# Interleaving a second stream with an LSTM: per-block multipliers and applies ahead of residual squares and statistics

## The chip, the cores and the metric

The kernel runs on one core of one Trainium2 chip. The metric is the device time of the program in microseconds (us). Before the change it took 1949.37 us, the median of three runs (1946.18 to 1950.16).

## The reference, cut to what matters

A batch of 128 graphs with 64 nodes and 256 features goes through four layers, each `x = x + layer(relu(layernorm(x)))` on the residual stream `x`: a batch-normed graph convolution, a graph convolution followed by LSTMs, an attention, and a masked attention. The change is inside the second layer:

```python
h = relu(layernorm(x))
u = relu(adj @ (h @ Wg0 + bg0)); u = relu(adj @ (u @ Wg1 + bg1))      # two graph convolutions
for p in range(1, 5):                                                 # four LSTMs, one after another
    g = x_t @ Wih[p-1].T + h @ Whh[p-1].T + bias                      # p steps per window of p nodes
    c = sigmoid(f) * c + sigmoid(i) * tanh(gg);  h = sigmoid(o) * tanh(c)
    u[:, last node of each window] = h of the last step
x = x + u
```

Each LSTM overwrites nodes that the next one reads, so the four follow each other.

## The kernel before, in words

All values are fp32. The 8192 rows (graph, node) of `x` are cut into 16 chunks of 512 rows. In the LSTM stage two chunks make a block, and the loop `for sc in range(last + 1)` of L1045 goes over the eight blocks. The input of a block's LSTMs is a tile `hT`, features on partitions and columns ordered by node and graph.

**The LSTM stream.** `lstm` (L676) builds matmuls on TensorE (PE) into PSUM banks, gates on ScalarE (ACT), cell and state updates on VectorE (DVE). For p = 1 a block is done in two parts of 512 columns. A part has six PSUM banks (gates i, g and o, called 0, 2 and 3, by two feature halves c) and 12 products of 512 columns (L790), which the profile shows as 24 matmuls, four to a bank. The banks have the tags y, z and x, two banks each, so part 1 reuses the banks of part 0, and p = 2 those of part 1: a matmul that opens a bank waits until ACT has read it. ACT reads a bank by a sigmoid or tanh (`first_acts`, L769). DVE then multiplies (`first_cell`, L775), ACT takes the tanh of the cell (L776), and DVE writes the new state into `hT` (`new_state`, L729). The ACT order of a part is gate 0, gate 2, two tanhs of the cell, gate 3. p = 2 runs its first products on halves of the nodes, 24 matmuls of 256 columns each: the first 24 need part 0's states alone, the other 24 part 1's.

**The other stream.** Every `yield` of `lstm` is a place, numbered n = 0 to 21 in a block: n = 0 and 1 lie in and after part 0 of p = 1, n = 2 and 3 in and after part 1, n = 4 inside the products of p = 2, n = 5 after its first step. At a place the loop takes one unit of other generators (L1069, L1070), in the order in which `units` entered them. The generators are:

- `residual` (L930) of the two chunks of the previous block: unit 0 transposes 32x32 squares on DVE (L936, four instructions into `hm`) and writes them to DRAM (`put`, L239); unit 1 reads them back into the dead `hT` (`get`, L246, four DMAs); unit 2 adds them to the residual `xs` (`add_squares`, L276).
- `convolutions` (L622) of the two chunks of the next block, 14 units: unit 0 scales and transposes (L542, L630), writes, reads back and loads `xs`; unit 1 adds squares to `xs` (L276); unit 2 takes the layernorm statistics (L165, L166, and a reciprocal root on GpSimd, POOL, L99 and L100); units 3 and 4 make the multiplier `nmr` on DVE (L183) and apply the layernorm on ACT in two halves (L185, two instructions each); unit 5 is a matmul with the adjacency (`agg_b`, L206), unit 6 copies its banks (L647), unit 7 multiplies by the weights (L557), and so on.
- `ahead` (L995) of the previous block's chunks, which prepares the next layer: put, read back, statistics (at n = 21), and, for the second chunk, in the following block under the name `LATE`: two applies (units 3 and 4: L183, then L185 into `h`) and unit 5, squares and put (L264, L239).

The order of all five engines is written by hand (`manual_schedule`, L1042): each engine runs its instructions in the order of the code, and a wait holds whatever is behind it on that engine. The DMAs here are issued from SyncE (SP), in order too. The tiles `hm`, `h2` and `nm` share one tag with three buffers.

## Time and profile before

| | value |
|---|---|
| time, median of 3 | 1949.37 us (1946.18 to 1950.16) |
| profiled execution: time, span, mean granted PE clock | 1950.89 us, 1949.1 us, 0.997 |
| PE busy | 1918.5 us, 98% of the span |
| DVE, ACT, POOL busy | 1143.4 us (59%), 947.3 us (49%), 367.8 us (19%) |
| blocks 2 to 6: start of p = 1 on PE | 608.41, 770.75, 931.37, 1091.94, 1254.20 us |

The page of the profile gives busy times by engine, and groups of instructions by source line with the idle time of the engine just before them and what ended it. A row of the timeline has the start, the length and the engine, then the source line, the operation, the tiles and the count of what was merged; a bracket at its end is the idle time of that engine just before, with its releaser. The waits view sums the idle time of one engine by line and releaser. The table by stretches gives busy time of each engine and the granted PE clock, 1.00 being full speed.

### The profile page before, as it was taken

The numbers are of one execution on the slowest core, as the hardware profiler recorded it, in microseconds if no ns is written. First come the engines' busy times: TensorE is split into PE (matmuls) and PEld (weight loads), VectorE is DVE, ScalarE is ACT, GpSimd is POOL, SyncE is SP. The second block draws the span as 40 slices with busy tenths as digits, with TensorE's granted clock in tenths as the row PEclk, the third lists the DMA queues.
The fourth block names the chain that finished last, engine by engine and source line by source line (L and its number), as shares of the span: only waits on it lengthen the run. The fifth ranks groups of instructions, "written<-read, shape, count | busy, mean of one in ns | idle before, by whom it ended". The sixth has DMA issues, their size and how long they took to land.

```text
span 1949.1 us, 37871 instructions
## 1 busy us (share of the span) xinstructions
PE 1918.5 (98%) x14839; PEld 1437.6 (74%) x14839; DVE 1143.4 (59%) x3000; ACT 947.3 (49%) x2120; POOL 367.8 (19%) x525
## 2 busy tenths in 40 slices
PE   9999999999999999999999999999999999999998
PEld 5444456896896898699689689879969966666665
DVE  6644454556556656655755754665555566566675
ACT  5654434455455455455544545535554544333443
POOL 2105211211211211121121121112112111111121
PEclk9999999999999999999999999999999999999999
DMA  4216712125324522531632542253144244444432
GB/s 135 61 36 228 281 34 80 67 82 191 124 82 160 176 82 80 177 109 65 213 112 82 179 157 82 101 169 108 58 150 129 86 150 122 131 134 138 140 117 82
DMA packets 109057, 238.23 MB, mean 122 GB/s; under 512 B 11216, under 2 KB 73168, under 8 KB 108880
## 3 DMA queue, kind: packets, MB, share of 16 engines
q1 hardware_dynamic: 108128, 234.47, 36.3%
q8 instruction: 117, 1.92, 0.4%
q0 software_dynamic: 320, 1.05, 0.2%
q14 instruction: 60, 0.49, 0.1%
q10 hardware_dynamic: 432, 0.30, 0.0%
HBM read 168.93 MB, written 66.85 MB: 121 GB/s over the span
## 4 chain that ended last, share of the span: by engine, by line
PE 88%; DVE 4%; ACT 3%; DMA 2%; issue 1%; POOL 1%; SPq 0%; DVEq 0%; ACTq 0%; POOLq 0%
PE x L826 22%; PE g L790 13%; PE z L826 11%; PE y L826 6%; PE z L369 6%; PE v L1095 5%; PE p_q L1102 5%; PE z L352 5%; PE p_k L1102 3%; PE u L571 3%; PE v L557 3%; DMA far_y<-ym 1%; PE agg_c L206 1%; PE s L1269 1%; PE o L1316 1%
## 5 line engine op out<-in xcount | busy, mean ns | idle before, releaser
L835 DVE TENSOR_TENSOR gates<-gates,x 128x128 f32<-128x128 f32 (+2 forms) x384 | 119.6, 323 | 344.9 <-PE x L826 343.0
L826 PE MATMUL x<-xd,wset 128*128 128x128 f32 (+2 forms) x1280 | 285.3, 311 | 0.1
L826 PE MATMUL x<-hd,wset 128*128 128x128 f32 (+2 forms) x1152 | 247.1, 303 | 0.0
L826 PEld LDWEIGHTS x<-xd,wset 128*128 128x128 f32 x1280 | 202.4, 190 | 17.0 <-DVE gates L835 3.0
L790 PE MATMUL g<-hT,wset 128*128 128x256 f32 (+2 forms) x744 | 191.8, 415 | 12.5 <-ACT gates L769 11.4
L718 ACT ACTIVATE gates<-gates,bias 128x256 f32<-128x256 f32 (+4 forms) x384 | 170.4, 491 | 66.5 <-DVE gates L835 63.7
L884 POOL TENSOR_TENSOR gates<-gates 128x512 f32<-128x512 f32 (+2 forms) x48 | 74.9, 1560 | 647.0 <-ACT gates L718 624.3
L826 PEld LDWEIGHTS x<-hd,wset 128*128 128x128 f32 x1152 | 185.3, 191 | 4.9
L790 PEld LDWEIGHTS g<-hT,wset 128*128 128x128 f32 x744 | 142.8, 195 | 60.6 <-ACT gates L769 17.5
L769 ACT ACTIVATE gates<-g,bias 128x512 f32<-128x512 f32 (+2 forms) x240 | 136.0, 608 | 103.7 <-PE g L790 100.4
L790 PE MATMUL g<-hT,wih 128*128 128x512 f32 x384 | 166.4, 593 | 0.0
L826 PE MATMUL z<-hs,wset 128*128 128x128 f32 (+2 forms) x768 | 154.2, 303 | 0.0
L832 ACT COPY gates<-y 128x128 f32<-128x128 f32 (+2 forms) x192 | 54.1, 293 | 205.6 <-PE y L826 205.1
L790 PEld LDWEIGHTS g<-hT,wih 128*128 128x128 f32 x384 | 72.5, 190 | 87.5 <-issue 82.9
L826 PEld LDWEIGHTS z<-hs,wset 128*128 128x128 f32 x768 | 119.9, 191 | 3.3
L352 PE MATMUL z<-agg,w_sb 128*128 128x512 f32 x256 | 114.1, 599 | 1.5 <-DVE agg L337 1.5
L775 DVE TENSOR_TENSOR cell<-gates 128x512 f32<-128x512 f32 (+2 forms) x80 | 50.0, 648 | 106.2 <-ACT gates L769 106.0
L369 PE MATMUL z<-h,w_sb 128*128 128x512 f32 x256 | 110.2, 593 | 0.0
L835 DVE TENSOR_TENSOR gates<-gates,z 128x128 f32<-128x128 f32 (+2 forms) x384 | 104.9, 317 | 0.1
L832 ACT COPY gates<-x 128x128 f32<-128x128 f32 (+2 forms) x192 | 56.4, 295 | 93.8 <-PE x L826 92.9
L718 ACT ACTIVATE gates<-x,bias 128x128 f32<-128x128 f32 (+2 forms) x192 | 74.7, 389 | 50.9 <-PE x L826 48.0
L826 PE MATMUL z<-hT,wset 128*128 128x128 f32 (+1 forms) x512 | 96.9, 302 | 0.0
(212 smaller groups left out, 3546.4 us busy)
## 6 DMA issues: line engine op xcount, KB each, us to landing
wset<-wfar SPq DMA_DIRECT2D x96, 960.0 KB, 6.3
hT<-far_h SPq DMA_DIRECT2D x116, 128.0 KB, 2.9
far_h<-hm SPq DMA_DIRECT2D x16, 512.0 KB, 5.6
far_n<-xs SPq DMA_DIRECT2D x16, 512.0 KB, 6.0
xs<-far_n SPq DMA_DIRECT2D x64, 128.0 KB, 2.9
far_x<-xs SPq DMA_DIRECT2D x16, 512.0 KB, 2.6
x<-far_x SPq DMA_DIRECT2D x64, 128.0 KB, 3.4
xt<-in_x_dram SPq DMA_DIRECT2D x15, 512.0 KB, 3.9
```

The costliest lines, as they stand in the source:

```text
L352: nc.tensor.matmul(ps, w1_sb[:, k, m * P : (m + 1) * P], agg[:, k, :], start=(k == 0), stop=(k == KD - 1))
L369: nc.tensor.matmul(banks[c, m], w2_sb[:, k, m * P : (m + 1) * P], h1[c][:, k, :], start=(k == 0), stop=(k == KH - 1))
L557: nc.tensor.matmul(banks[m], wg0_sb[:, k, m * P : (m + 1) * P], agg[:, k, :], start=(k == 0), stop=(k == KD - 1))
L718: nc.scalar.activation(gate(q, c, part), src, AF.Tanh if q == 2 else AF.Sigmoid, bias=bs[:, q * KD + c : q * KD + c + 1])
L769: nc.scalar.activation(columns_of(gate(q, c)), natural(banks[q, c][:, :n].rearrange("p (w b) -> p w b", b=nb)), AF.Tanh if q == 2 else AF. ...
L790: nc.tensor.matmul(banks[q, c][:, :n].rearrange("p (w b) -> p w b", b=nb)[:, w, :], block(q, c, k), hv[:, k, w.start * p : (w.stop - 1) * ...
L826: nc.tensor.matmul(folded(self.psum(kind)), wsets[p, self.q][:, BLOCKS[kind][i], :], (ox[self.s] if part == "x" else oh)[kind], start=firs ...
L832: nc.scalar.copy(gate(self.q, kind // 5, halves[kind // 5]), self.psum(kind))
L835: nc.vector.tensor_add(gate(self.q, *dst), gate(self.q, *a), self.psum(kind))
L884: nc.gpsimd.tensor_mul(gates[:, 0, :, :n], gates[:, 0, :, :n], gates[:, 2, :, :n])
L1095: nc.tensor.matmul(ps[:, i, :], hT[:, k, j, :], w[:, k, first : first + D], start=(k == 0), stop=(k == KD - 1))
L1102: nc.tensor.matmul(ps.rearrange("p (a n) -> p a n", n=P), w[:, k, m * P : (m + 1) * P], hT[:, k], start=(k == 0), stop=(k == KD - 1))
```

## The change

Only the tables of places and the order of entering change; no instruction is added, removed or altered.

```diff
-    RESIDUAL = (0, 2, 3), (1, 3, 4)
-    CONV = (1, 1, 2, 3, 4, 4, 5, 6, 7, 8, 9, 10, 10), (3, 5, ...
+    RESIDUAL = (0, 2, 3), (1, 3, 5)
+    CONV = (1, 2, 3, 3, 4, 4, 5, 6, 7, 8, 9, 10, 10), (3, 5, ...
-    LATE = 1, 1, 2
+    LATE = 1, 1, 3
...
+            if sc > 1:
+                units(LATE[:2], aheads[sc * SUP - 3])
+            if sc < last:
+                for i in range(SUP):
+                    units((CONV if sc else FIRST)[i], convs[(sc + 1) * SUP + i])
+                new_hT(sc + 1)
             if sc:
                 for i in range(SUP):
                     units(RESIDUAL[i], residual((sc - 1) * SUP + i, hTs[sc - 1]))
             else:
                 units([0], convs[1])
-            if sc < last:
-                for i in range(SUP):
-                    units((CONV if sc else FIRST)[i], convs[(sc + 1) * SUP + i])
-                new_hT(sc + 1)
             if sc > 1:
-                units(LATE, aheads[sc * SUP - 3])
+                units(LATE[2:], aheads[sc * SUP - 3])
```

By place (blocks 2 to 6; "first" and "second" are the two chunks of a block):

| n | before | after |
|---|---|---|
| 1 | second residual's squares and put; first convolution's add, statistics; late applies | late applies; first convolution's add; second residual's squares and put |
| 2 | first residual's read back; first convolution's apply, half 1; late squares and put | first convolution's statistics; first residual's read back |
| 3 | first residual's add; second residual's read back; first convolution's apply, half 2; second convolution's unit 0 | first convolution's apply, both halves; second convolution's unit 0; first residual's add; second residual's read back; late squares and put |
| 4 | second residual's add; then as before the adjacency matmul and its copies | the adjacency matmul and its copies |
| 5 | second convolution's add | second convolution's add; second residual's add |

It is meant to let the multipliers and applies, which ACT needs, go before work of DVE that nothing waits for soon. The lines of the changed kernel below L1052 stand three further down than those named here.

## The prediction, made before the changed kernel was run

> **What bounds the kernel now.** I read the page, then the waits of PE, then the timelines of PE, ACT and DVE around the longest wait, then the granted clock by stretches. Part 1 of the page:

> ```profile
> PE 1918.5 (98%) x14839; PEld 1437.6 (74%) x14839; DVE 1143.4 (59%) x3000; ACT 947.3 (49%) x2120; POOL 367.8 (19%) x525
> ```

> PE is the bound; time can only come from its gaps or its clock. The waits of PE from 250 us on (engine, line and tile that waited, what it waited for, total us, times, longest):

> ```profile
> PE g L790 <- ACT gates L769: 11.4, 5, 2.3
> PE y L826 <- ACT gates L769: 2.1, 2, 1.3
> PE agg_b L206 <- ACT cv L176: 1.3, 2, 1.1
> ```

> Five equal gaps carry most of it. One lies in each of the blocks 2 to 6, none in block 1. PE in block 4:

> ```profile
> 943.82 8.32 PE L790 MATMUL g<-hT,wih 128*128 128x512 f32 x19
> 951.97 1.94 PE L790 MATMUL g<-hT,wset 128*128 128x256 f32 x8
> 956.18 6.45 PE L790 MATMUL g<-hT,wset 128*128 128x256 f32 x28 [2.27 <-ACT gates L769]
> ```

> After p = 1 (wih), p = 2 gets eight matmuls out, into the y and z banks, and then stands 2.27 us for an x bank. ACT in the same stretch:

> ```profile
> 941.87 0.69 ACT L769 ACTIVATE gates<-g,bias 128x512 f32<-128x512 f32 x1 [0.78 <-PE g L790]
> 948.80 2.07 ACT L185 ACTIVATE h<-xs,nmr_n,rstd_n 128x256 f32<-128x256 f32 x4 [6.24 <-DVE nmr_n L183]
> 950.77 2.39 ACT L769 ACTIVATE gates<-g,bias 128x512 f32<-128x512 f32 x4
> 953.34 1.23 ACT L776 ACTIVATE gates<-cell 128x512 f32<-128x512 f32 x2 [0.18 <-DVE cell L775]
> 954.48 1.08 ACT L185 ACTIVATE cv<-xs,nmr_b,rstd_b 128x256 f32<-128x256 f32 x2
> 955.47 1.24 ACT L769 ACTIVATE gates<-g,bias 128x512 f32<-128x512 f32 x2
> ```

> ACT stood 6.24 us before the late applies, waiting for one 128x4 multiplier; the gates of part 1 queue behind them, and two more applies (954.48) come before gate 3, whose first half ends at 956.16: that frees the x bank. Why the multiplier was late, on DVE:

> ```profile
> 941.80 1.49 DVE L729 TENSOR_TENSOR hT<-gates 128x512 f32<-128x512 f32 x2
> 943.20 2.08 DVE L936 STREAM_TRANSPOSE hm<-hT 128x256 f32<-128x256 f32 x4
> 945.21 1.25 DVE L276 TENSOR_TENSOR xs<-xs,cv 128x512 f32<-128x512 f32 x2
> ...
> 948.63 0.13 DVE L183 SCALAR_TENSOR_TENSOR nmr_n<-mv_n,rstd_n 128x4 f32<-128x4 f32 x1
> ```

> It stands behind squares, an add and statistics (946.49 to 948.71), although its own inputs were complete when POOL finished rstd_n at 938.31 (937.27 + 1.04). Last, the granted clock (PEclk, third number from the right) in 8 us from the end of each gap, blocks 2 to 6:

> ```profile
> 633.20:641.20 8.00, 7.98 (x31) 6.31 (x32) 7.80 (x10) 1.52 (x3) 4.18 (x4) 0.79 0.51 156
> 795.50:803.50 8.00, 7.94 (x94) 6.63 (x95) 7.92 (x11) 1.57 (x4) 4.18 (x4) 1.00 0.52 157
> 956.10:964.10 8.00, 7.92 (x94) 6.61 (x95) 7.90 (x11) 1.59 (x4) 4.19 (x4) 1.00 0.50 155
> 1116.70:1124.70 8.00, 7.94 (x28) 6.31 (x28) 7.79 (x10) 1.56 (x4) 4.19 (x4) 0.79 0.50 155
> 1279.00:1287.00 8.00, 7.98 (x40) 6.55 (x44) 7.80 (x10) 1.53 (x3) 4.18 (x4) 0.80 0.51 156
> ```

> Three of the five gaps are followed by a slow clock. The stretches between them, from 450 to 1949 us, read 1.00.

> [...] ACT ran nothing for 6.24 us while part 1's first bank was ready. [...] here gaps of 2.27 us are followed by a drop in three of five. [...] the adds of L276 took 2.36 us for two at 957.38 beside POOL's work, 1.25 us without; I use the slow figure where POOL is busy.

> **The change, part by part.** PE's and POOL's orders are the same in both builds; ACT's differs only in that gate 3 of part 1 stands ahead of the first two convolution applies (blocks 1 to 6). The rest is DVE's and SP's order. I walk block 4, with everything up to 941.8 as it was.

> *Late applies first.* DVE writes the multiplier right after the state update, 943.29 to 943.42. ACT applies 943.45 to 945.5 (2.07). Part 1's banks are finished on PE at fixed times: 48 matmuls of p = 1 take 931.37 to 951.97, 0.429 each, 1.717 per bank, so part 1, which begins at 941.67, completes its banks at 943.39, 945.10, 946.82, 948.54, 950.25 and 951.97; ACT starts 0.20 later at best (the bracketed reads of part 0 do). Gate 0 then runs 945.5 to 946.75, gate 2 at 947.0 to 947.7 and 948.75 to 949.45.

> *Add and squares behind it.* The add needs `xs`, whose DMA landed at 943.06: 943.4 to 944.65; four transposes to 946.75, before the first cell product can start at 947.9. They cost nothing. The second product ends at 950.3 and its tanh at 951.1.

> *Gate 3 ahead of the convolution's applies.* First half 951.1 to 951.75, second (bank complete 951.97) 952.2 to 952.85. PE wants the two x banks at 951.97 + 1.84 = 953.8 and 954.3. Margins 2.05 and 1.45 us: the gap goes. Removed: 5 x 2.27 = 11.35 us.

> *Statistics at place 2, both applies at place 3.* DVE 950.3 to 952.45 (2.14), which puts the state update at 952.45 to 953.75; PE needs it after 24 matmuls of 0.228 at 957.45. POOL's root takes 1.36, to 953.85; multiplier 954.0; four applies to 956.1. The adjacency matmul comes after 36 matmuls, at 960.2: margin 4.1 us. Cost nothing; PE's own 24 matmuls hide it.

> *The heap at place 3 on DVE.* Scaling 1.0 to 1.82, transposes 1.3, residual add 1.25 to 2.36, late squares 1.42; with the slow figures 954.0 to 960.9. The copies of L647 wait for the adjacency matmul anyway (961.3) and end at 962.7; their consumer L557 ran at 968.94, now 966.7: margin 4 us. The residual add needs a read back: its write was issued at 941.9 and took 8.2 us, read back landed 954.1; DVE comes to it at 957.1.

> *SP.* The second read back now queues behind unit 0's write (2.7 us to landing, as at 962.85 before) and loads: issued about 962, landed about 967. Its add sits at place 5, when DVE is done with 969.0 (971.27 less 2.27), and with two adds of 1.3 DVE is free at 971.6; the next product it is needed for was at 977.39, now 975.1: margin 3.5 us.

> *Clock.* If the drops follow the gaps, they go too. Their cost is the longer run of the same 28 matmuls: from the end of the gap to the first weight load of `agg_b`, 7.96, 8.07 and 7.76 us in blocks 2, 5 and 6 against 6.38 in block 3: 1.58 + 1.69 + 1.38 = 4.65 us.

> Sum: 11.35 + 4.65 = 16.0 us. Taken off the profiled execution, 1950.89, it gives 1934.9; off the median it gives 1933.4. How many drops the median run had I can't see. I take 1934.

> **The rivals.** *The gap goes, the clock drops stay* (they come from load, not from the gap): 1949.4 - 11.35 = 1938.0. For it: DMA runs at 0.50 to 0.52 in those stretches. Against: it does so with and without a drop. *Part of the gap stays*: `xs` landed just 0.34 us before DVE wants it; the slowest such load took 6.5 us against 4.8 here. DVE, and through the cell products ACT, would then be about 1.4 us late, within the margin on the first bank; a delay of 3 us would leave about 1 us in five blocks, and clock drops in some: about 1942. *A new wait takes its place (slower)*: the applies, late by the statistics, hold the adjacency matmul, or the crowded places 3 and 5 hold L557 or the products of p = 2. It has to eat a margin of 3.5 to 4.1 us and then cost more than 3.2 us a block, so one of my times would have to be 7 us off; five waits of 5 us in place of the 16 give 1958. *Nothing moves*: another engine frees the x bank equally late; nothing in the trace points to one: 1949.

> **How the numbers follow.** Forecast 0.73; clock drops stay 0.10; part of the gap stays 0.09; no change 0.03; slower 0.05. The range begins at 1931, three below the forecast (the spread of the runs before, 1946.18 to 1950.16, is as much below its median), and ends at 1942, which takes in the next two cases. Faster by over 0.2% (below 1945.5): 0.92; within: 0.03; slower: 0.05.

> **What would show it.** In the profile after: no wait of L790 on L769 in blocks 2 to 6; ACT's applies into `h` at 12 us from the start of p = 1 in place of 17.4; gate 3 of part 1 read by 21.5 us; blocks of about 158 us from start to start, as block 1 has (157.7); mean clock 1.00. It would be wrong if L206, L557 or L826 showed new waits on ACT or DVE, or if the mean clock stayed at 0.997 without gaps.

## The result, and the profile after

The changed kernel takes 1932.61 us (median of 4 runs, 1932.41 to 1932.70), beside 1948.05 us for the kernel before (median of 4 runs, 1946.18 to 1950.16). The ratio is 0.992, 95% interval 0.9903 to 0.9937: faster by 0.8%. The forecast was 1934.

Part 1 of the page of the changed kernel, with busy us and share of the span by engine:

```profile
PE 1912.5 (99%) x14839; PEld 1435.4 (74%) x14839; DVE 1141.9 (59%) x3000; ACT 949.4 (49%) x2120; POOL 364.3 (19%) x525
```

The same instructions, and the busy times of DVE and ACT within 2.1 us of those before; the span is 1930.6 us in place of 1949.1. The waits of PE from 250 us on (who waited, for what, total us, times, longest):

```profile
PE y L826 <- ACT gates L769: 2.1, 2, 1.3
```

The line that led this list, L790 waiting 11.4 us for L769, is gone; the next one stands as it stood, and so does that of L206 for L176 (1.3 us). PE in block 4, whose p = 1 now starts at 924.05:

```profile
924.05 20.77 PE L790 MATMUL g<-hT,wih 128*128 128x512 f32 x48
944.65 7.93 PE L790 MATMUL g<-hT,wset 128*128 128x256 f32 x36
952.52 1.16 PE L206 MATMUL agg_b<-adjt_bd,cv 64*64 64x64 f32 x64
```

The 8 and the 28 matmuls that had a gap between them are now one row of 36. ACT in the same stretch:

```profile
936.08 2.07 ACT L185 ACTIVATE h<-xs,nmr_n,rstd_n 128x256 f32<-128x256 f32 x4 [0.83 <-DVE nmr_n L183]
...
943.40 0.67 ACT L769 ACTIVATE gates<-g,bias 128x512 f32<-128x512 f32 x1
944.86 0.69 ACT L769 ACTIVATE gates<-g,bias 128x512 f32<-128x512 f32 x1 [0.78 <-PE g L790]
947.92 2.08 ACT L185 ACTIVATE cv<-xs,nmr_b,rstd_b 128x256 f32<-128x256 f32 x4 [2.38 <-DVE nmr_b L183]
```

The late applies start 12.03 us after the start of p = 1 (forecast: 12; before: 17.4), after a wait of 0.83 us in place of 6.24. The two halves of gate 3 are read at 944.07 and 945.55, that is 20.0 and 21.5 us after the start (forecast: 21.5 for the later). PE wants the x banks after 8 matmuls of p = 2; 36 of them took 944.65 to 952.52, 0.2186 each, so at 946.40, and the second bank after two more, at 946.84. The margins are 2.3 and 1.3 us. DVE, just ahead of that:

```profile
935.88 0.16 DVE L183 SCALAR_TENSOR_TENSOR nmr_n<-mv_n,rstd_n 128x4 f32<-128x4 f32 x1
936.31 1.29 DVE L276 TENSOR_TENSOR xs<-xs,cv 128x512 f32<-128x512 f32 x2 [0.27 <-DMA xs<-in_x_dram]
937.52 2.10 DVE L936 STREAM_TRANSPOSE hm<-hT 128x256 f32<-128x256 f32 x4
```

The multiplier comes first, then the add and the squares. The add even waits 0.27 us for its load, since DVE now reaches it sooner; nothing is behind it that PE needs at once.

From start to start of p = 1, in us:

| block | 1 | 2 | 3 | 4 | 5 | 6 |
|---|---|---|---|---|---|---|
| before | 157.84 | 162.34 | 160.62 | 160.57 | 162.26 | 161.95 |
| after | 157.85 | 157.89 | 157.84 | 158.20 | 157.84 | 157.84 |

Blocks 2 to 6 lose 18.13 us of the 18.5 us by which the two profiled spans differ; the next largest part is 0.44 us in block 7. The mean granted clock is 1.00 (before: 0.997).

### The profile page after: what moved, and what is told of

Same layout as the page of the kernel before. It is cut to its first block, busy times and chain, and to the rows that moved or that the text cites. A ratio compares the mean times of both kernels' runs of the same rounds, so it can differ in the third digit from the quotient of the medians.

```text
span 1930.6 us, 37895 instructions
## 1 busy us (share of the span) xinstructions
PE 1912.5 (99%) x14839; PEld 1435.4 (74%) x14839; DVE 1141.9 (59%) x3000; ACT 949.4 (49%) x2120; POOL 364.3 (19%) x525
## 4 chain that ended last, share of the span: by engine, by line
PE 95%; DVE 3%; ACT 1%; POOL 1%; issue 0%; DVEq 0%; POOLq 0%; ACTq 0%
PE x L826 22%; PE g L790 17%; PE z L826 11%; PE v L1098 6%; PE y L826 6%; PE z L369 6%; PE p_q L1105 5%; PE z L352 5%; PE p_k L1105 3%; PE u L571 3%; PE v L557 3%; PE agg_c L206 1%; PE s L1272 1%; PE o L1319 1%; PE tr L1132 1%; PE o L1219 1%
## 5 line engine op out<-in xcount | busy, mean ns | idle before, releaser
L835 DVE TENSOR_TENSOR gates<-gates,x 128x128 f32<-128x128 f32 (+2 forms) x384 | 119.6, 323 | 334.2 <-PE x L826 332.3
L826 PE MATMUL x<-xd,wset 128*128 128x128 f32 (+2 forms) x1280 | 285.1, 311 | 0.3 <-DVE gates L835 0.2
L826 PE MATMUL x<-hd,wset 128*128 128x128 f32 (+2 forms) x1152 | 246.8, 303 | 0.0
L826 PEld LDWEIGHTS x<-xd,wset 128*128 128x128 f32 x1280 | 202.1, 190 | 17.4 <-DVE gates L835 3.5
L826 PEld LDWEIGHTS x<-hd,wset 128*128 128x128 f32 x1152 | 185.1, 191 | 5.0
L769 ACT ACTIVATE gates<-g,bias 128x512 f32<-128x512 f32 (+2 forms) x240 | 138.0, 609 | 98.0 <-PE g L790 94.7
L790 PE MATMUL g<-hT,wset 128*128 128x256 f32 (+2 forms) x744 | 184.4, 405 | 1.2 <-DVE hT L729 1.1
L790 PEld LDWEIGHTS g<-hT,wset 128*128 128x128 f32 x744 | 140.5, 190 | 44.1 <-issue 8.8
L790 PE MATMUL g<-hT,wih 128*128 128x512 f32 x384 | 166.4, 592 | 0.0
L826 PE MATMUL z<-hs,wset 128*128 128x128 f32 (+2 forms) x768 | 154.1, 303 | 0.0
L790 PEld LDWEIGHTS g<-hT,wih 128*128 128x128 f32 x384 | 72.3, 190 | 87.7 <-issue 83.2
L826 PEld LDWEIGHTS z<-hs,wset 128*128 128x128 f32 x768 | 119.8, 191 | 3.3
L775 DVE TENSOR_TENSOR cell<-gates 128x512 f32<-128x512 f32 (+2 forms) x80 | 50.5, 649 | 101.0 <-ACT gates L769 100.9
L835 DVE TENSOR_TENSOR gates<-gates,z 128x128 f32<-128x128 f32 (+2 forms) x384 | 104.8, 318 | 0.1
L826 PE MATMUL z<-hT,wset 128*128 128x128 f32 (+1 forms) x512 | 96.9, 301 | 0.0
```

The source lines that it names most:

```text
L769: nc.scalar.activation(columns_of(gate(q, c)), natural(banks[q, c][:, :n].rearrange("p (w b) -> p w b", b=nb)), AF.Tanh if q == 2 else AF. ...
L790: nc.tensor.matmul(banks[q, c][:, :n].rearrange("p (w b) -> p w b", b=nb)[:, w, :], block(q, c, k), hv[:, k, w.start * p : (w.stop - 1) * ...
L826: nc.tensor.matmul(folded(self.psum(kind)), wsets[p, self.q][:, BLOCKS[kind][i], :], (ox[self.s] if part == "x" else oh)[kind], start=firs ...
L835: nc.vector.tensor_add(gate(self.q, *dst), gate(self.q, *a), self.psum(kind))
```

## The experiments

Two theories stood against each other on the order of work. One: all that counts is when ACT has read gate 3 out of the x bank, and the late multiplier's place sets it. The other: the remaining moves (gate 3 ahead of the convolution applies, the heaps at places 3 and 5) are part of the gain. On the clock: drops follow gaps, or they come from the load of the transfers. In the diffs that start from the kernel before, the minus lines are its own.

### The late multipliers and applies first, and nothing else

```diff
 # from the kernel before
+            if sc > 1:
+                units(LATE[:2], aheads[sc * SUP - 3])
...
-                units(LATE, aheads[sc * SUP - 3])
+                units(LATE[2:], aheads[sc * SUP - 3])
```

> Before, with one edit: the late applies (units 3 and 4 of the second chunk's generator) stand first at place 1; squares, statistics and the order of gate 3 and the convolution's applies stay. Theory (the late multiplier alone makes the gap): gate 3 of part 1 is read by 21.3 us after the start of p = 1 and PE wants the bank at 22.4, so the five gaps and the clock drops go; 1932 to 1934 us, as with the whole change. Rival (gate 3 must also stand ahead of the convolution's applies, or the crowded DVE order matters): gaps of 0.5 to 1.5 us stay, 1936 to 1942.

Measured: 1932.66 us (1932.39 to 1933.42), ratio to before 0.992, interval 0.9905 to 0.9936. Blocks 2 to 6 take 158.38, 157.82, 157.83, 157.82 and 157.84 us. ACT in block 4:

```profile
936.71 2.08 ACT L185 ACTIVATE h<-xs,nmr_n,rstd_n 128x256 f32<-128x256 f32 x4 [0.83 <-DVE nmr_n L183]
...
944.59 1.09 ACT L185 ACTIVATE cv<-xs,nmr_b,rstd_b 128x256 f32<-128x256 f32 x2 [0.46 <-DVE nmr_b L183]
945.59 1.24 ACT L769 ACTIVATE gates<-g,bias 128x512 f32<-128x512 f32 x2
```

Two convolution applies still stand ahead of gate 3, yet its halves are read by 946.26 and 946.83. p = 2 starts at 945.29 here, so PE wants the two banks at 947.04 and 947.48: margins of 0.8 and 0.65 us. This one move is enough for the whole gain.

### All the other moves, with the late multipliers entered last

```diff
 # from the changed kernel
-            if sc > 1:
-                units(LATE[:2], aheads[sc * SUP - 3])
...
-                units(LATE[2:], aheads[sc * SUP - 3])
+                units(LATE, aheads[sc * SUP - 3])
```

> The changed kernel with the late multipliers and applies entered last again at place 1, behind the first convolution's add and the second residual's squares; the statistics at place 2, gate 3 ahead of the convolution applies, and all other moves stay. Theory (what counts is when gate 3 has read the x bank, and either half of the change can bring that forward enough): the multiplier now comes after the state update, the add (1.29 us) and the squares (2.08 us) but no longer after the statistics, about 1.8 us sooner than before; the chain of gates moves up by that, and gate 3 by another 1.1 us for the two applies that it passes, 2.9 us in all, against a gap that cost 2.74 us. So the gap goes, or up to 0.3 us of it stays: blocks of 157.9 to 158.3 us, 1932.5 to 1935 us, no clock drops. Rival (the late multiplier has to be first, the other moves bring only what gate 3's place alone brought): blocks near 159.6 us, 1940 to 1943 us.

Measured: 1933.0 us (1932.78 to 1933.25), ratio 0.9916, interval 0.9901 to 0.9931. Blocks 2 to 6 take 157.89, 157.83, 158.18, 157.84 and 157.83 us, those of the changed kernel to 0.02 us; the 0.4 us more in the median do not come from them. ACT in block 4:

```profile
939.71 2.07 ACT L185 ACTIVATE h<-xs,nmr_n,rstd_n 128x256 f32<-128x256 f32 x4 [4.01 <-DVE nmr_n L183]
...
945.40 1.25 ACT L769 ACTIVATE gates<-g,bias 128x512 f32<-128x512 f32 x2
949.81 2.08 ACT L185 ACTIVATE cv<-xs,nmr_b,rstd_b 128x256 f32<-128x256 f32 x4 [3.16 <-DVE nmr_b L183]
```

Here ACT still stands 4.01 us for the late multiplier, which now has the add and the squares ahead of it but no longer the statistics; and gate 3 has no applies ahead of it. Its halves are read at 946.07 and 946.65; p = 2 starts at 945.12, and PE wants the banks at 946.87 and 947.31. Margins 0.8 and 0.7 us: no gap. So the other moves are enough too. The gains of the two halves of the change overlap and do not add up; together they only widen the margin, to 2.3 and 1.3 us.

### Only gate 3 ahead of the convolution applies

```diff
 # from the kernel before
-    CONV = (1, 1, 2, 3, 4, 4, ...
+    CONV = (1, 1, 3, 3, 4, 4, ...
```

> Before, with one edit: the first convolution's first apply moves from place 2 to place 3, so that gate 3 of part 1 stands ahead of both applies on ACT; the late multiplier stays behind squares and statistics. Theory: ACT still stands 6.2 us before the late applies; gate 3 comes about 1.0 us earlier, so gaps of about 1.3 us stay in five blocks: 5 us off, and fewer clock drops; 1939 to 1944. Rival (this reordering is the part that counts): 1932 to 1935.

Measured: 1941.69 us (1940.90 to 1942.55), ratio 0.9965, interval 0.9953 to 0.9977. PE in block 4:

```profile
952.46 6.46 PE L790 MATMUL g<-hT,wset 128*128 128x256 f32 x28 [1.29 <-ACT gates L769]
```

The two applies that gate 3 passes are 1.08 us of ACT; each gap shrinks from 2.27 to 1.29 us. The rest of the gap needs an earlier multiplier. No gap is followed by a drop of the clock: the blocks take 159.59 to 159.71 us, all five. (The mean clock of this execution, 0.999, is lost outside them, from 269.72 to 273.13 us and at the end.)

### The gap made again by another cause, in three lengths

Extra sigmoids on ACT, into a part of the tile `gates` that p = 1 does not read, ahead of gate 3 in part 1 of blocks 2 to 6. Everything else is the changed kernel.

```diff
 # from the changed kernel; 8 here, 6 and 12 in the other two
         if p == 1:
+            if name[0] in "23456" and name.endswith("_1"):
+                for _ in range(8):
+                    nc.scalar.activation(gates[:, 1, 0, :], gates[:, 0, 0, :], AF.Sigmoid)
             first_acts(3)
```

Eight:

> After, with eight sigmoids of 128x512 (0.6 us each) of a gate into a part of the tile that p = 1 does not read, ahead of gate 3 of part 1 in blocks 2 to 6: the gap of PE is made again at the same place and about as long (2.3 us), with the new order of DVE and SP. Theory (a gap of this length can drop the clock): the five gaps cost 2.7 us each, 1946 us, and in some runs the mean clock falls below 1.00 with 1.6 us for each drop, so the runs scatter from 1946 to 1950. Rival (the drops came from the load of DMA and DVE in the old order): all runs at 1946 with a clock of 1.00.

Measured: 1953.48 us (1951.74 to 1957.10), ratio 1.0028, interval 1.0019 to 1.0038. Five gaps of 2.73 us, longer than the 2.3 us that were meant. So the time missed the expected 1946 to 1950: a block with a gap and no drop takes 3.1 to 3.4 us more than in the changed kernel, not 2.7. Busy time and, third from the right, the granted clock in 8 us from the end of the gaps of blocks 2, 3 and 5; the number after it is the busy share of the DMA engines:

```profile
633.70:641.70 8.00, 7.97 (x23) 6.51 (x24) 7.55 (x13) 2.63 (x5) 3.47 (x4) 0.62 0.16 66
797.60:805.60 8.00, 7.98 (x94) 6.65 (x95) 7.84 (x14) 2.62 (x5) 3.46 (x4) 1.00 0.17 68
...
1120.20:1128.20 8.00, 7.99 (x28) 6.34 (x28) 7.54 (x13) 2.62 (x5) 3.47 (x4) 0.79 0.17 68
```

Two of the five gaps are followed by a drop (blocks 4 and 6 read 1.00, as block 3), with the DMA engines at 0.16 to 0.17. In the kernel before they were at 0.50 to 0.52, and in the run with gate 3 alone they were, behind the gaps, at 0.49 to 0.52 without a drop. So the load of the transfers is not what takes the clock.

Six:

> The changed kernel with six extra sigmoids on ACT (128x512 each, into an unused buffer) in part 1 of blocks 2 to 6, two fewer than in the run with eight. Each costs about 0.62 us on ACT, so the gap shrinks from 2.7 us to about 1.5 us. Theory (a drop of the clock needs a gap of about 2 us or more): no drop after any of the five gaps; gap plus refill 2.0 us a block, blocks of 159.7 to 160.0 us, 1942 to 1944 us, spread under 2 us. Rival (gaps of any length are followed by drops with the same chance as before, two or three of five): another 3 to 5 us, 1945 to 1949 us, and a spread of some 4 us.

Measured: 1941.41 us (1941.26 to 1942.42), ratio 0.9962, interval 0.9948 to 0.9976. PE in block 4, and the other four alike:

```profile
951.64 6.46 PE L790 MATMUL g<-hT,wset 128*128 128x256 f32 x28 [1.41 <-ACT gates L769]
```

Five gaps of 1.41 us, no drop after any: blocks of 159.65 to 159.99 us. The median is 0.6 us below the expected range, since I had put the cost of a gap at 2.0 us; four of the five blocks take 1.81 to 1.86 us more than the 157.84 of block 1, 0.4 to 0.45 beyond the idle time. The rival, the same chance of a drop after any gap, does not hold.

Twelve:

> The changed kernel with twelve extra sigmoids on ACT in part 1 of blocks 2 to 6. The gap grows to about 5.2 us, with the refill 5.9 us a block. Theory (a longer gap makes a drop more likely): drops after four or all of the five gaps, 1.4 to 1.7 us each or more: blocks of 163.7 us without and 165.4 us with a drop, 1968 to 1972 us. Rival (a drop follows two or three gaps of five whatever their length): 1964.5 to 1967.5 us.

Measured: 1972.32 us (1970.77 to 1972.54), ratio 1.0116, interval 1.0101 to 1.0131. Block 4:

```profile
969.32 8.02 PE L790 MATMUL g<-hT,wset 128*128 128x256 f32 x28 [5.37 <-ACT gates L769]
```

Five gaps of 5.37 us, and a drop after each: the 28 matmuls take 8.62, 9.32, 8.02, 8.87 and 7.79 us where they take 6.46 at full clock, 10.3 us more in all. 1932.6 + 5 x (5.37 + 0.45) + 10.3 = 1972.0, as measured. The drops are longer than I had said, 1.3 to 2.9 us each.

### The gap kept, but filled with work for PE

In the kernel before, 18 transposes of the identity, which nothing reads, go just ahead of the first product that waits for an x bank, in blocks 2 to 6.

```diff
 # from the kernel before, in the loop over products
+                if p == 2 and i == 0 and at == 4 and name[0] in "23456":
+                    keep_busy(18, f"g{name}")
                 nc.tensor.matmul(
```

> Before, with 18 transposes of the identity (0.12 us each, 2.15 us) into a spare bank ahead of the first matmul on an x bank in p = 2, blocks 2 to 6: PE works through the gap, nothing becomes earlier. Theory: PE's wait there falls below 0.4 us, the clock stays at 1.00 in every run, and all runs lie near 1946 (after plus 5 x 2.7), without the scatter of the runs before. Rival (drops come from load): runs scatter from 1946 to 1950 and the mean clock falls below 1.00 as before.

Measured: 1947.18 us (1946.82 to 1948.47, 12 runs), ratio 0.9996, interval 0.9987 to 1.0004. PE in block 4:

```profile
953.02 2.13 PE L157 MATMUL idle_g<-ident 128*128 128x128 f32 x18
955.46 6.45 PE L792 MATMUL g<-hT,wset 128*128 128x256 f32 x28 [0.31 <-ACT gates L769]
```

The product that waits starts as late as before: the blocks take 160.58 to 160.79 us, all five the length that a block with a gap and no drop had before (160.57 and 160.62). The drops are gone after all five gaps, though nothing but the transposes was added, and no run of the twelve has a mean clock below 0.999. So it is PE's idle time, 2.27 us a gap before and 0.31 here, that brings them. The median is 0.9 us above the 1946.3 that the kernel before takes without a drop (worked out below); the profiled execution has a wait of 0.9 us for a load after the LSTM stage, which the profile of before has not, and no run shows whether the transposes bring it. Against the kernel before the median moves by less than the interval can tell from none, but the runs now lie within 1.65 us, while 23 runs of the kernel before on the same chip lay between 1945.85 and 1951.66.

## Why the prediction was right, point by point

**The cause** was right: one 128x4 multiplier, ready on its inputs, stood behind work of DVE that nothing waited for, and through ACT's queue, which stood 6.24 us for it in block 4, held gate 3, and gate 3 the x bank (2.27 us of PE). The run with that one move shows it, and the run with all the others shows something that the prediction did not say: its second step, gate 3 ahead of the applies together with the statistics moved back, would, by that run's trace, have been enough without the first.

**The size of the gap was too small.** The step "Removed: 5 x 2.27 = 11.35 us" took the idle time of PE's row for its cost. A gap without a drop costs 160.57 - 157.84 = 2.73 us (157.84 is block 1, where the prediction had 157.7), so five cost 13.7. In block 4 of before, the matmul behind the gap was due 8 x 0.2186 after 951.97, at 953.72, and came at 956.18: 2.46 us, since the row counts from the modelled end of the matmul before, 953.91, which reaches past that start. The other 0.27 us lie in the 28 matmuls themselves, by their beginning, where the weight loads wait once more, for the second x bank:

```profile
956.76 5.48 PEld L790 LDWEIGHTS g<-hT,wset 128*128 128x128 f32 x26 [0.28 <-ACT gates L769]
```

The 28 matmuls took 6.39 us to the first load of `agg_b`, in place of 28 x 0.2186 = 6.12. Idle time plus about 0.45 also fits the gaps of 1.29 us (1.75 us a block at the least) and of 1.41 us (1.81 to 1.86), and two of the three gaps of 2.73 us without a drop (3.13 and 3.14 us more than the same blocks of the changed kernel; 3.41 in block 3).

**The clock** was right: the drops belong to the gaps. Why only three of the five gaps of 2.27 us were followed by one, the prediction had not worked out; the last section reads it from the traces. The forecast took 4.65 us for three; by the lengths of the blocks they were 4.75 (162.34, 162.26 and 161.95, each less 160.6).

**The sum** was 16.0 us, where the two profiled executions differ by 18.5: 13.7 + 4.8 + 0.4 of block 7, less 0.4 for block 4, which takes 158.20 us after, with a new wait of 0.2 us of L826 for L835. For the median the sum had two errors that partly cancel. It left out 2.3 us of the gaps, and it took off three drops where the usual run before has fewer: without any drop in these blocks the kernel before takes 1932.6 + 13.7 = 1946.3 us, its fastest runs are at 1945.85 to 1946.35, and its medians, 1948.05 to 1949.37, have room for one or two. That leaves 0.8 us. Taking 1934, between the 1933.4 from the median and the 1934.9 from the profiled execution, added 0.6: together the 1.4 us by which the forecast is high. That the two errors partly cancel is luck: neither follows from the other.

**Margins.** The add's load (the rival in which part of the gap stays) held DVE for 0.27 us, which cost PE nothing. The convolution's applies ended 25.95 us after the start of p = 1, where the walk had 24.7. The one step of the walk that failed is "POOL's root takes 1.36". POOL and DVE in block 4 of the changed kernel:

```profile
945.06 0.59 POOL L99 TENSOR_SCALAR rstd_b<-mv_b 128x4 f32<-128x4 f32 x1 [14.07 <-DVE mv_b L166]
945.73 1.43 POOL L100 TENSOR_TENSOR rstd_b<-rstd_b,mhalf 128x4 f32<-128x4 f32 x1
```

```profile
944.89 1.38 DVE L729 TENSOR_TENSOR hT<-gates 128x512 f32<-128x512 f32 x2
947.20 0.69 DVE L183 SCALAR_TENSOR_TENSOR nmr_b<-mv_b,rstd_b 128x4 f32<-128x4 f32 x1 [0.93 <-POOL rstd_b L100]
```

The root took 2.10 us, 945.06 to 947.16, beside DVE's state update, and the multiplier 0.69 beside POOL's next work; before, with DVE idle, L100 took 1.04 us and the same multiplier 0.15. The prediction had seen two adds of DVE take 2.36 us beside POOL's work and 1.25 us without; it used the slow figures for the heap at place 3 and not for the root. The runs with sigmoids move the root and the state update apart: gate 3 is late there, and with it the state update. POOL in block 4 of the run with six:

```profile
948.74 0.23 POOL L99 TENSOR_SCALAR rstd_b<-mv_b 128x4 f32<-128x4 f32 x1 [14.07 <-DVE mv_b L166]
949.05 1.04 POOL L100 TENSOR_TENSOR rstd_b<-rstd_b,mhalf 128x4 f32<-128x4 f32 x1
```

The state update follows at 951.62, after 2.96 us in which DVE is idle. With DVE idle the root takes 1.35 us again, 948.74 to 950.09, as in the kernel before (948.80 to 950.15); beside the state update it takes 2.10 us in all five blocks 2 to 6 of the changed kernel. So the overlap with the state update is what lengthens it; what the two share there, no run isolates, and why the multiplier takes 0.69 us beside POOL's next work is not shown. Spans on POOL are rough. The two took 1.2 us of the margin; the adjacency matmul itself came 0.4 us sooner than the walk had it, and about 2.5 of the forecast 4.1 were left there. L557 and place 5 of DVE kept 3.8 and 3.65 us (forecast: 4 and 3.5).

**The rivals** fell one by one: the clock is at 1.00, no part of the gap is left, and the only new wait is the one of 0.2 us.

## What to carry to other kernels

When a small result is late and its inputs were not, look at what stands ahead of it in its engine's queue, and enter first what another engine's queue is waiting for. Cost a gap of PE by comparing two equal stretches of the program with and without it, not by the idle time of its row (2.73 us against 2.27 here), and ask of each clock drop behind it whether it is part of the gap's price. Two edits that bring the same event forward don't add up: once the buffer is free in time, more margin brings no time (1932.66 us with margins of 0.8 and 0.65 us in block 4, 1932.61 with 2.3 and 1.3).

## What the runs showed of the hardware

How often a gap of PE was followed by a drop of the granted clock, by its length (five gaps in each kernel):

| kernel | idle before the 28 matmuls, us | drops |
|---|---|---|
| gate 3 alone | 1.29 | 0 |
| six sigmoids | 1.41 | 0 |
| before | 2.27 | 3 |
| eight sigmoids | 2.73 | 2 |
| twelve sigmoids | 5.37 | 5 |
| before, gap filled | 0.31 | 0 |

Here is the kernel before at its gap in block 2, and then the run with eight sigmoids at its gap in block 2, in steps of 3.41 us whose edges are those of the drops (PE's busy time comes first, the clock is third from the right):

```profile
630.19:633.61 3.42, 1.15 (x6) 0.60 (x4) 2.57 (x8) 3.24 (x7) 0.00 (x0) 1.00 0.15 55
633.61:637.02 3.41, 3.41 (x10) 2.60 (x9) 3.41 (x5) 1.11 (x3) 3.05 (x3) 0.50 0.93 257
```

```profile
629.61:633.02 3.41, 1.39 (x7) 0.88 (x5) 0.00 (x0) 3.25 (x7) 1.17 (x2) 1.00 0.02 6
633.02:636.44 3.42, 2.71 (x6) 2.18 (x7) 2.73 (x4) 2.03 (x5) 1.96 (x3) 0.50 0.00 0
636.44:639.85 3.41, 3.41 (x9) 2.70 (x8) 3.38 (x6) 1.28 (x3) 1.51 (x2) 0.50 0.07 28
```

An estimate from these numbers: a gap of up to about 1.7 us brings no drop in this kernel, one of more than about 4 us always does, since no edge can split it into parts below 2.02 us, and between them it is the place of the edge that decides. No run here shifts the edges on purpose; they are read from the traces.

The drops also account for the scatter of the kernel before: it spreads over 5.8 us (mean granted clock 0.996 in the run of 1951.66 us, 1.000 in that of 1945.85), and with its gaps filled over 1.65, and the changed kernel's runs over 0.3.
